# Grouped logits in stacked pairs on eight accumulation banks, and the grouped normaliser in SBUF

## The chip, the cores and the metric

The kernel runs on one core of one Trainium2 chip. The metric is device time in microseconds (us); the kernel before takes 3412.44 us, the median of three runs (3412.42 to 3412.56). A core has a matrix engine (PE, whose weight loads the profile shows as PEld), a vector engine (DVE), a scalar engine (ACT), a slower elementwise engine (POOL) and a queue that issues DMAs (SP). Each works through its own list of instructions in order, and waits on semaphores for the others. PE writes only to PSUM, which here is eight banks of 128 partitions by 512 float32 (2 KB a partition each).

## The reference

Four cross-attention layers are applied in sequence to `x` (4 batches, 512 queries, 256 channels), with the same context `ctx_2048` (4, 1024 keys, 512). Layers 0, 2 and 3 ("masked") have 16 heads of 64; a few key columns get a bias made of two query masks. Layer 1 ("grouped") has an RMS norm ahead, 16 query heads of 16 over 4 key/value heads. Cut to what matters:

```python
def masked(hidden, ctx, mask_A, mask_B, Wq, Wk, Wv, Wo, bo, tokens_A, tokens_B):   # layers 0, 2, 3
    q, k, v = heads_of_64(hidden @ Wq), heads_of_64(ctx @ Wk), heads_of_64(ctx @ Wv)
    logits = einsum('bhqd,bhkd->bhqk', q, k) * 64 ** -0.5 + col_bias   # bias on tokens_A, tokens_B
    out = einsum('bhqk,bhkd->bhqd', softmax(logits), v)
    return merge(out) @ Wo + bo + hidden

def grouped(x, cond, wq, wk, wv, wo, norm_w):                          # layer 1
    q = heads_of_16(rmsnorm(x, norm_w) @ wq)                           # 16 heads, 4 per key head
    scores = einsum('btgrd,bsgd->bgrts', q, k) * 16 ** -0.5
    return x + merge(einsum('bgrts,bsgd->btgrd', softmax(scores), v)) @ wo
```

All is float32.

## The kernel before, in words

**Units and steps.** Work is cut into units of two heads: 8 units for each layer and batch. A unit's logits are 8 blocks of 128 keys by 1024 (two heads of 512 queries), kept in SBUF in one of three sets (`g.st[0..7]`, and a ninth place `g.mx`). `order()` lays the units out in 96 steps: every step has one masked unit `g`, and 32 of them also a grouped unit `lam`: steps 12 to 19, 22 to 29, 32 to 39 and 68 to 75. `coming` is the grouped unit of the step after. Everything below concerns the 28 steps that have both `lam` and `coming` (12-18, 22-28, 32-38, 68-74). Of these, the 16 even ones make values for a pair of masked units (`v_pair`, L605, eight items), the 12 odd ones keys (`k_part`, L552, eight items). Four of the even ones (16, 26, 36, 72) also have a grouped output projection.

**What one such step does on PE, in order.** (1) `scores(g)`: eight tiles of masked logits (L869, the first with a small bias product, L875), each in a place of two banks, copied to SBUF by ACT (L879). (2) `attend` (L902) of the masked unit of the step before, with a place of one bank. (3) A list `fill` of items: output projections (L1108), the next queries (L766), then values or keys, until their estimated times reach 8.0 or 9.5; then `sums_beside` (L1074, the masked unit's softmax sums) and `attend_grouped` (L902 again, 128 by 32 products, into a place of one bank that `keep_even` (ACT, L912) and `keep_odd` (DVE, L916) empty). (4) The grouped logits of `coming`: `logits_pair` (L842) makes two blocks from four products of 32 rows each, which PE runs side by side, in two places of two banks. There are four such pairs. A planner with due times (`pairs`, 12 + 2.5 i) puts the first after `attend_grouped`, and each other one behind one more item of values or keys.

**After a pair.** ACT copies each block to SBUF (L848), which frees its banks, and DVE takes the block's maximum (`block_max`, L926). Behind the fourth pair, `max_quarters` (L942 to L953, seven small DVE instructions in one more PSUM bank) and `max_everywhere` (L966) make the maximum over all keys; POOL subtracts it in the next step (L972). Behind `attend_grouped` of every second grouped unit (`h` = 1, the odd steps), `turn_grouped` divides the unit's output by its sums: three DVE instructions over a PSUM bank (L1029 to L1031) and a product (L1035).

**Banks.** `Place` gives banks out while the program is built. It takes the free place that was given back longest ago in program order, not in time. In these steps two-bank places come from banks 0 to 5, those of `logits_pair` (`last=2`) from banks 0 to 3; one-bank places come from banks 4 to 7. An instruction that reuses a bank waits until the last reader of that bank has finished.

```python
    def max_quarters(g):
        ...
            w = Place(1)
        quarter, half = w.ap[:, 0:32], w.ap[0:64, 32:64]
```

## Time and profile before

| what | value |
|---|---|
| median of three runs | 3412.44 us |
| profiled execution: its time / its span | 3414.65 us / 3412.9 us |
| PE busy | 3397.2 us (100%) |
| DVE / POOL / ACT busy | 2957.4 us (87%) / 2594.2 us (76%) / 2348.5 us (69%) |
| granted PE clock | 0.999 |

A row of a group or a timeline gives the start (timelines only), the duration, the engine, the line of the kernel, the operation with its tiles and shapes, and the count of instructions merged. Matmuls are pipelined, so starts are compared with starts. A float32 product of the kernel is two PE instructions, so a pair of four products shows as x8. The span starts with the first instruction; the profiled execution's time has 1.75 us more than its span.

### The profile page before, as it was taken

How to read it: one execution, taken by the hardware profiler on the slowest of the kernel's cores; microseconds unless marked ns; L12 is line 12 of the kernel's file. 1: busy time of each engine (PE TensorE's matmuls, PEld its weight loads, DVE VectorE, ACT ScalarE, POOL GpSimd, SP SyncE). 2: the span in 40 equal slices, each digit the busy share in tenths (PEclk: the TensorE clock that was granted, in tenths of full speed). 3: DMA queues.
4: the chain of work that ended last, by engine and by line, in shares of the span. 5: the costliest groups of instructions: out<-in, count | busy, mean ns of one | idle time of the engine just before them, and what ended most of it. 6: DMA issues, size and time to landing. Idle time of an engine off the chain costs nothing.

```text
span 3412.9 us, 42703 instructions
## 1 busy us (share of the span) xinstructions
PE 3397.2 (100%) x15520; PEld 1651.6 (48%) x15520; DVE 2957.4 (87%) x3871; ACT 2348.5 (69%) x2729; POOL 2594.2 (76%) x1337
## 2 busy tenths in 40 slices
PE   9999999999999999999999999999999999999999
PEld 5555444444444444445455454554444445454554
DVE  7888799988999889987988889888899988889887
ACT  5666688776787768876666666666678776666665
POOL 4888588875888768888668768677588888769675
PEclk9999999999999999999999999999999999999999
DMA  3232211011101121001001110011111101011100
GB/s 103 69 109 82 65 38 51 30 48 38 55 27 30 48 62 30 27 30 54 19 28 53 35 47 31 28 53 56 38 30 52 36 21 53 28 48 49 34 30 10
DMA packets 147733, 151.69 MB, mean 44 GB/s; under 512 B 23608, under 2 KB 125496, under 8 KB 147012
## 3 DMA queue, kind: packets, MB, share of 16 engines
q1 hardware_dynamic: 144958, 140.58, 13.2%
q0 software_dynamic: 2560, 8.39, 0.8%
q8 instruction: 123, 2.02, 0.2%
q14 instruction: 86, 0.70, 0.1%
q10 hardware_dynamic: 6, 0.00, 0.0%
HBM read 132.15 MB, written 15.73 MB: 43 GB/s over the span
## 4 chain that ended last, share of the span: by engine, by line
PE 93%; DVE 5%; ACT 1%; issue 1%; POOL 0%; DMA 0%; DVEq 0%; ACTq 0%; POOLq 0%
PE ps L902 21%; PE ps L665 18%; PE ps L869 18%; PE ps L552 9%; PE ps L605 9%; PE ps L1108 5%; PE ps L766 5%; PE ps L842 4%; DVE ps L886 2%; DVE st L974 1%; PE ps L1074 1%; PE ps L567 1%; PE ps L875 1%; ACT st L879 1%; PE ps L781 0%
## 5 line engine op out<-in xcount | busy, mean ns | idle before, releaser
L1019 POOL TENSOR_TENSOR st<-st 128x1024 f32<-128x1024 f32 x668 | 1582.2, 2369 | 562.8 <-ACT st L980 518.3
L980 ACT ACTIVATE st<-st 128x1024 f32<-128x1024 f32 x1024 | 1042.1, 1059 | 228.0 <-POOL st L972 118.0
L974 DVE TENSOR_TENSOR st<-st,ps 128x1024 f32<-128x1024 f32 x768 | 884.3, 1215 | 3.3
L902 PE MATMUL ps<-st,v 128*64 128x512 f32 (+1 forms) x4064 | 789.8, 595 | 0.0
L972 POOL TENSOR_TENSOR st<-st 128x1024 f32<-128x1024 f32 x256 | 598.1, 2379 | 211.9 <-DVE st L966 106.0
L879 ACT COPY st<-ps 128x1024 f32<-128x1024 f32 x768 | 713.1, 1050 | 55.3 <-PE ps L875 55.2
L886 DVE TENSOR_TENSOR ps<-ps,st 128x1024 f32<-128x1024 f32 x420 | 517.9, 1233 | 212.3 <-ACT st L879 174.6
L926 DVE TRANSPOSE_TENSOR_REDUCE tops<-st 128x32 f32<-128x1024 f32 x544 | 628.4, 1212 | 69.3 <-ACT st L848 64.6
L869 PE MATMUL ps<-qt,kt 64*128 64x512 f32 x3008 | 687.2, 596 | 0.0
L902 PEld LDWEIGHTS ps<-st,v 128*64 128x64 f32 (+1 forms) x4064 | 239.8, 130 | 535.2 <-issue 448.6
L869 PEld LDWEIGHTS ps<-qt,kt 64*128 64x128 f32 x3008 | 280.4, 186 | 345.5 <-ACT st L879 147.6
L605 PE MATMUL ps<-wv,ctx 128*128 128x256 f32 x1344 | 313.7, 385 | 1.1 <-ACT ctx L428 1.1
L665 PE MATMUL ps<-st 128*128 128x128 f32 (+1 forms) x1620 | 308.8, 339 | 3.7 <-ACT ps L688 3.4
L552 PE MATMUL ps<-ctx,wk 128*128 128x512 f32 x672 | 310.8, 603 | 0.2 <-ACT ctx L428 0.2
L605 PEld LDWEIGHTS ps<-wv,ctx 128*128 128x128 f32 x1344 | 251.0, 191 | 93.1 <-issue 54.9
L848 ACT COPY st<-ps 128x1024 f32<-128x1024 f32 x256 | 247.0, 1018 | 62.3 <-PE ps L842 58.4
L665 PEld LDWEIGHTS ps<-st 128*128 128x128 f32 x1620 | 214.3, 192 | 96.3 <-issue 86.6
L680 ACT COPY st<-ps 128x512 f32<-128x512 f32 x45 | 26.4, 586 | 339.2 <-PE ps L665 339.2
L552 PEld LDWEIGHTS ps<-ctx,wk 128*128 128x128 f32 x672 | 121.7, 189 | 181.0 <-issue 163.6
L766 PE MATMUL ps<-x,wq 128*128 128x512 f32 x376 | 180.4, 602 | 1.3 <-ACT x L391 1.1
L1108 PE MATMUL ps<-ot,wo 128*128 128x512 f32 x380 | 173.2, 598 | 0.0
L842 PE MATMUL ps<-qt,kt 32*128 32x512 f32 x1024 | 160.0, 640 | 0.0
(200 smaller groups left out, 2955.8 us busy)
## 6 DMA issues: line engine op xcount, KB each, us to landing
wv<-in_L_xattn_Wv_dram SPq DMA_DIRECT2D x48, 512.0 KB
ctx<-kept SPq DMA_DIRECT2D x24, 1024.0 KB
wk<-in_L_xattn_Wk_dram SPq DMA_DIRECT2D x47, 512.0 KB
wo<-in_L_xattn_Wo_dram SPq DMA_DIRECT2D x96, 128.0 KB
wq<-in_L_xattn_Wq_dram SPq DMA_DIRECT2D x94, 128.0 KB
st<-kept SPq DMA_DIRECT2D x4, 2048.0 KB
qt<-q SPq DMA_DIRECT2D x64, 128.0 KB
kept<-st SPq DMA_DIRECT2D x12, 512.0 KB
```

What stands on the lines that cost most here:

```text
L552: nc.tensor.matmul(m, lhsT=g.w["k"][:, k, :], rhs=ctx_half[g.b, n][:, k, :], start=(k == 0), stop=(k == KT - 1),)
L605: nc.tensor.matmul(m[:, half * 2 * P : (half + 1) * 2 * P], lhsT=ctx_half[g.b, t // 4][:, k, t % 4 * P : (t % 4 + 1) * P], rhs=g.w["v2"][: ...
L665: nc.tensor.matmul(m if is_keys else m[:, q], lhsT=right[:, k, :] if is_keys else left_[:, k, q], rhs=left_[:, k, :] if is_keys else right ...
L869: nc.tensor.matmul(m[:, j * S : (j + 1) * S], lhsT=g.kt[g.rows[j], keys], rhs=g.qt[g.rows[j], :], start=True, stop=t > 0,)
L879: nc.scalar.copy(g.st[t], m)
L886: nc.vector.tensor_tensor(top, top, g.st[t], ALU.max)
L902: nc.tensor.matmul(g.po[at, :], lhsT=g.v[:, t, rows], rhs=g.st[t][:, j * S : (j + 1) * S], start=(t == first), stop=(t == last),)
L926: nc.vector.tensor_reduce(out_, of.rearrange("p (b x) -> p b x", x=32), AX.X, op, apply_transpose=True)
L972: nc.gpsimd.tensor_tensor(g.st[t], g.st[t], g.mb, ALU.subtract)
L974: nc.vector.tensor_tensor(g.st[t], g.st[t], g.mb, ALU.subtract)
L980: nc.scalar.activation(st, st, AF.Exp)
L1019: nc.gpsimd.tensor_tensor(g.acc, g.st[0] if t == 1 else g.acc, g.st[t], ALU.add)
```

## The change

In the 28 steps, the four pairs of grouped logits are no longer spread by due times. Two pairs stand directly behind `attend_grouped`, then two items of values or keys, then the other two pairs. Their banks come from a fixed list, `PAIR_BANKS`: the first two pairs on banks 0-3 and 4-7, the others on banks 2-5 and 6, 7, 0, 1. The one-bank places of the values or keys behind each two pairs come from a list of hints: banks 0, 1, then 2, 3. `max_quarters`, which is called inside the second two pairs, finds the list empty and takes its bank by the old rule. An odd number of value or key items ahead of the first pairs is made even: in the odd steps and in steps 16, 26, 36 and 72 one item more stands before `attend_grouped`. The exponential of the masked unit's last block moves from behind the first pair to behind the second. `turn_grouped` works in `g.mx` (SBUF) in place of the PSUM bank, which `keep_odd` now always gives back.

```diff
-        def __init__(self, width=2, last=2, among=(4, 5, 6, 7)):
+        def __init__(self, width=2, last=2, among=(4, 5, 6, 7), at=None):
             free = given_back
-            if width == 2:
+            if at is not None or width == 1 and hinted:
+                at = hinted.pop(0) if at is None else at
+            elif width == 2:
...
-    def logits_pair(g, i):
-        ws = [Place(), Place()]
+    PAIR_BANKS = ((0, 2), (4, 6), (2, 4), (6, 0))
+
+    def logits_pair(g, i, fixed):
+        ws = [Place(at=PAIR_BANKS[i][odd] if fixed else None) for odd in range(2)]
...
         nc.vector.tensor_tensor(half, half, g.po[64:128, :], ALU.add)
-        if g.h == 0:
-            g.place.back()
+        g.place.back()
...
     def turn_grouped(g):
-        normalise_grouped(g, g.place.ap)
-        g.place.back()
+        normalise_grouped(g, g.mx[:, 0:S])
...
-            logits_pair(coming, i)
-            if by_ones and events:
+            logits_pair(coming, i, bool(lam))
+            if by_ones and events and i == (1 if lam else 0):
                 events.pop(0)[2]()
...
-            while where < len(fill) and total < (8.0 if by_ones and of_values else 9.5):
+            enough = 8.0 if coming and of_values else 9.5
+            while where < len(fill) and total < enough:
                 total += fill[where][0]
                 where += 1
+            if coming:
+                where += sum(each in of_values + of_keys for each in fill[:where]) % 2
+
+                def two_pairs(bank):
+                    hinted.clear()
+                    pair(pairs.pop(0)[1])
+                    pair(pairs.pop(0)[1])
+                    hinted.extend(range(bank, bank + 2))
+
+                fill.insert(where + 2, (2.0, lambda: two_pairs(2)))
+                fill.insert(where, (2.0, lambda: two_pairs(0)))
             fill.insert(where, (3.6, attend_grouped))
...
-            while pairs and pairs[0][0] <= now:
+            while pairs and not lam and pairs[0][0] <= now:
...
         while pairs:
             pair(pairs.pop(0)[1])
+        hinted.clear()
```

More of the change, by code (lines that the diff above doesn't have):

```diff
@@ L101 @@
     tabled = [False]
+    hinted = []
     class Place:
-        def __init__(self, width=2, last=2, among=(4, 5, 6, 7)):
+        def __init__(self, width=2, last=2, among=(4, 5, 6, 7), at=None):
             free = given_back
-            if width == 2:
+            if at is not None or width == 1 and hinted:
+                at = hinted.pop(0) if at is None else at
+            elif width == 2:
                 whole = [n for n in range(0, 8, 2) if n in free and n + 1 in free]
@@ L1444 @@
             of_queries.append((1.7, lambda: project_q(follows)))
+        of_keys = []
         if fast_k:
@@ L1458 @@
         else:
-            fill += of_queries
-            if kk:
-                fill += keys(*kk)
+            of_keys = keys(*kk) if kk else []
+            fill += of_queries + of_keys
         of_values = values(g) if g and g.n % 2 == 0 and not fast_v else []
```

## The prediction

> **What bounds the kernel.** I read the page first (busy shares, chain of waits), then PE's timeline, then those of ACT, DVE and POOL in one even and one odd step, and last PE's own waits. The page:

> ```profile
> PE 3397.2 (100%) x15520; PEld 1651.6 (48%) x15520; DVE 2957.4 (87%) x3871; ACT 2348.5 (69%) x2729; POOL 2594.2 (76%) x1337
> ...
> PE 93%; DVE 5%; ACT 1%; issue 1%; POOL 0%; DMA 0%; DVEq 0%; ACTq 0%; POOLq 0%
> ```

> PE has about 16 us idle in 3412.9, so a microsecond added to or taken from PE's list is a microsecond of the result. PE's timeline from the first grouped pair of an even step (14 us):

> ```profile
> 450.88 1.14 PE L842 MATMUL ps<-qt,kt 32*128 32x512 f32 x8
> 451.95 1.99 PE L605 MATMUL ps<-wv,ctx 128*128 128x256 f32 x8
> 453.88 1.33 PE L842 MATMUL ps<-qt,kt 32*128 32x512 f32 x8
> 455.14 1.99 PE L605 MATMUL ps<-wv,ctx 128*128 128x256 f32 x8
> 457.06 1.15 PE L842 MATMUL ps<-qt,kt 32*128 32x512 f32 x8
> ...
> 463.25 1.13 PE L869 MATMUL ps<-qt,kt 64*128 64x512 f32 x4
> 464.22 0.38 PE L875 MATMUL ps<-aug_q,aug_k 64*128 64x512 bf16 x2
> 464.43 6.17 PE L869 MATMUL ps<-qt,kt 64*128 64x512 f32 x28
> ```

> From start to start a pair costs 1.07 or 1.26, an item behind it 1.92. The same items in a row (32 of them from 439.30 to 446.30) cost 1.75 each, so a change of product shape costs about 0.17. The pairs at 1.26 (1.35 in odd steps) wait 0.2 to 0.3 for a copy that frees one of their four banks. Next DVE and ACT in the same stretch, and DVE and POOL in an odd step:

> ```profile
> 451.63 0.69 DVE L916 TENSOR_TENSOR o<-o,ps 64x512 f32<-64x512 f32 x1 [1.73 <-ACT o L912]
> 453.15 2.37 DVE L926 TRANSPOSE_TENSOR_REDUCE tops<-st 128x32 f32<-128x1024 f32 x2 [0.82 <-ACT st L848]
> ...
> 462.34 2.37 DVE L926 TRANSPOSE_TENSOR_REDUCE tops<-st 128x32 f32<-128x1024 f32 x2 [0.63 <-ACT st L848]
> 464.75 0.61 DVE L942 TENSOR_REDUCE ps<-tops 128x32 f32<-128x256 f32 x1
> ...
> 466.25 0.38 DVE L953 TENSOR_TENSOR every<-ps,other_max 64x32 f32<-64x32 f32 x2
> 466.74 1.25 DVE L966 STREAM_TRANSPOSE st<-every 128x1024 f32<-128x1024 f32 x1
> 467.91 4.58 DVE L926 TRANSPOSE_TENSOR_REDUCE tops<-st 128x32 f32<-128x1024 f32 x4
> ```

> ```profile
> 452.10 1.93 ACT L848 COPY st<-ps 128x1024 f32<-128x1024 f32 x2 [0.50 <-PE ps L842]
> 453.92 1.07 ACT L980 ACTIVATE st<-st 128x1024 f32<-128x1024 f32 x1
> ```

> ```profile
> 486.78 17.05 POOL L1019 TENSOR_TENSOR st<-st 128x1024 f32<-128x1024 f32 x7
> ```

> The reader is to see that L942 to L953 (the small maximum in a PSUM bank) end at 466.63, 3.4 us after the next step's first score tile starts. Today they use bank 6 or 7 here, which no score tile uses, so nothing on PE waits for them.

> **The change, part by part.** T is the start of the first pair; all step times are from T. The kernel before starts the second score tile of the next step at T + 13.55 in the 12 plain even steps (464.43 - 450.88), at T + 15.31 in the odd ones (14.13 to the first tile, 1.18 on), and at T + 15.36 in the four even steps with a projection.

> *Stacking, what it saves.* The instruction orders of the two kernels show two shape changes in place of four. Four products side by side stream at 0.43 (L902's 32 products of 128 by 32 take 3.57, so eight take 0.89), so the second pair of a stack would cost 0.87 in place of a pair at 1.07 to 1.35. Two items behind a stack cost 1.92 + 1.75 = 3.67 in place of 3.85. Without any wait, an even step would shrink from 12.37 to 2 x (1.07 + 0.87 + 3.67) = 11.2.

> *Wait 1, the grouped output's bank.* The bank that `place_out` gives the grouped output is 7, 6 or 4, and the second pair now wants all of banks 4-7. Its product there waits for L916, which ends at 452.32, T + 1.44. With 0.1 for the release and 1.02 for the last product (a held-up pair ends so much after its release), the items start at T + 2.55, not 1.94; bank 0, which they need, is free by then (first copy ends at T + 2.2). PE's queue behind that product is everything, so 0.6 is lost. The second stack starts at T + 2.55 + 3.67 = T + 6.22. It needs bank 0 again: the item's copy, behind the moved exponential (1.07), ends near T + 6.9, when the fourth pair gets there at T + 7.1. Nothing is lost, with 0.2 to spare.

> *Wait 2, the bank of the small maximum.* Inside the second stack the give-back order hands `max_quarters` bank 4, and in all 28 following steps a score tile is placed on banks 4, 5 directly behind banks 0, 1 (in steps 14 and 74 first of all). In the program of the changed kernel that tile waits for the second half of L953. When does it end? The stack's first copy starts 1.22 after the stack (452.10 - 450.88), its first maximum 1.05 later (453.15): T + 8.49. Four maxima in a row take 4.58. From the last maximum's end (464.71) to the end of L953 (466.63) is 1.92. So bank 4 is free at T + 14.99 and the tile starts at T + 15.07. PE would be there sooner: the items behind the second stack wait for bank 2 until T + 8.5, the first tile starts at T + 12.2, the second could at T + 13.35. PE waits 1.7. Behind it is all of PE's list; DVE, ACT and POOL then stand 2 us earlier against PE, so nothing else turns late and nothing is given back.

> *Sum without the turn.* Plain even steps: 15.07 - 13.55 = +1.52, 12 times, 18.2. In the other 16, one item more (1.75) stands ahead of T. Even with projection: 16.82 - 15.36 = +1.46, 4 times, 5.8. Odd: the item pairs cost 3.65, so 1.75 + 15.05 = 16.80, less 15.31 = +1.49, 12 times, 17.9. Steps 13 and 73 have transposes or a store ahead and the bank-4 tile first: 0.3 more each. Sum +42.5.

> *The turn in SBUF.* L1029 to L1031 work from SBUF to SBUF: 711 to 727 ns either way (L807 against L1029), so nothing. The product L1035 (688 ns) now reads both inputs from SBUF, while POOL is in its seven adds. In an odd step DVE goes from L916 to its first maximum in 3.15, then does eight in 9.13: the bank is free at T + 15.03 by this way too, so each microsecond more here is one on PE. The rows bound it: no delay (L830, both inputs in SBUF, 748 ns, POOL idle), or a whole POOL add of 2.37 waited for. Of the two nearest rows L1035 lacks the second SBUF input and L830 lacks a busy POOL, so neither speaks for its end; I take half an add, 1.2, 12 times: +14.4. Ends 0 and 28.4.

> [...]

> [...]

> *All else*: the four last grouped steps (19, 29, 39, 75) only move the turn, under DVE's idle time. DMAs and POOL's list are the same. **Sum: +42.5 + 14.4 = +56.9.** On the profiled execution 3414.65 this is 3471.6; that execution is 2.2 above the median, so against the median: 3469.

> **Rivals.** *A, the bank comes in time (other side).* If four maxima and L942 to L953 took under 4.8 in place of 6.5 behind the second stack's first copy, wait 2 would go. Then the first tile starts at T + 12.2 in place of 12.37, and about 0.17 to 0.28 is won per step: 3406. Without wait 1 as well (items from T + 2.28, when bank 0 is free, 0.27 sooner in 28 steps): 3398; with no wait at all, 3380. For it: DVE idles 0.6 to 0.8 between maxima today. Against: the copies of one stack come every 0.97, faster than maxima (1.14), so four queue up. *B, dearer.* If the turn is delayed by a whole add and the second pair restarts as a pair of its own (1.07 + 0.2 more, 28 times, 5 us): 3412.4 + 42.5 + 28.4 + 5 = 3488. Against: POOL's adds start at a fixed distance. *C, wait 2 alone*, the turn free: 3455; this is the low end of the forecast. *D, it cancels*: the shape changes might cost more than 0.17; to cancel +42.5, stacks would have to save 1.5 more each step than the 1.16 of the ideal. Not likely.

> **How the numbers follow.** Forecast (waits 1 and 2, any turn between C and a full add: 3455 to 3483) 0.88; A 0.04; B 0.05; D 0.03. Two runs of this kernel can be told apart from about 0.2%, 7 us. Faster 0.04, same 0.03, slower 0.93. The range: C's 3455 less 0.3 of wait 1 and 0.2 of DVE's chain in 28 steps, 14, gives 3441; the full add gives 3483.

> **What would show it.** In the profile after: PE's first idle time in score tiles, 28 waits of 1.5 to 3 us for the line of L953; PE busy below 98.5%; pairs as x16 from start to start 1.9 (no wait 1) or 2.55; L1035's duration far over 688 in odd steps if the turn is held. The prediction is wrong if those 28 waits are missing, or if the stall is given back where today's kernel waits on something that I take for PE's own work.

## The result, and the profile after

The changed kernel takes 3489.11 us, the median of four runs (3486.09 to 3491.34); the kernel before beside it took 3412.43 us. The ratio is 1.0223, interval 1.0210 to 1.0235: slower by 76.7 us, where 56.6 were predicted. The direction is right, the time is 20 us above the forecast and 6 us above the range's upper end. The profiled execution took 3486.09 us with a span of 3484.0 us, which is 71.1 us more than the span before. In the changed file the lines of the code have moved by three to five: L842 is L847, L869 is L874, L916 is L921, L926 is L930, L953 is L957, L1035 is L1038.

The page after: busy times, the chain of waits by engine, and the group of the score tiles.

```profile
PE 3398.3 (98%) x15520; PEld 1665.5 (48%) x15520; DVE 2971.0 (85%) x3871; ACT 2344.9 (67%) x2729; POOL 2593.5 (74%) x1337
...
PE 84%; DVE 13%; ACT 2%; issue 1%; POOL 0%; DMA 0%; DVEq 0%; ACTq 0%
...
L874 PE MATMUL ps<-qt,kt 64*128 64x512 f32 x3008 | 702.3, 607 | 61.3 <-DVE every L957 61.3
```

PE does the same work in nearly the same busy time, and what was added is, by these sums, idle time. (The sums hide two opposite changes: the pairs and the items between them take less, and the score tiles 702.3 us where they took 687.2.) The list of PE's waits (total, times, longest) names it:

```profile
PE ps L874 <- DVE every L957: 61.3, 28, 3.2
PE ps L608 <- ACT st L853: 4.7, 16, 0.3
PE ps L555 <- ACT st L853: 3.5, 12, 0.3
```

These are the 28 waits of the prediction, one for each step, for the small maximum. PE's timeline of an even step, the same one that the prediction shows, and DVE's beside it:

```profile
449.06 2.61 PE L847 MATMUL ps<-qt,kt 32*128 32x512 f32 x16
451.60 3.72 PE L608 MATMUL ps<-wv,ctx 128*128 128x256 f32 x16
455.25 2.00 PE L847 MATMUL ps<-qt,kt 32*128 32x512 f32 x16
457.55 3.72 PE L608 MATMUL ps<-wv,ctx 128*128 128x256 f32 x16 [0.29 <-ACT st L853]
461.20 1.13 PE L874 MATMUL ps<-qt,kt 64*128 64x512 f32 x4
462.16 0.38 PE L880 MATMUL ps<-aug_q,aug_k 64*128 64x512 bf16 x2
464.18 6.28 PE L874 MATMUL ps<-qt,kt 64*128 64x512 f32 x28 [1.64 <-DVE every L957]
```

```profile
457.53 4.62 DVE L930 TRANSPOSE_TENSOR_REDUCE tops<-st 128x32 f32<-128x1024 f32 x4 [1.58 <-ACT st L853]
462.25 0.59 DVE L946 TENSOR_REDUCE ps<-tops 128x32 f32<-128x256 f32 x1
...
463.74 0.38 DVE L957 TENSOR_TENSOR every<-ps,other_max 64x32 f32<-64x32 f32 x2
```

The two stacks of pairs are shorter, as predicted: 2.54 from start to start with wait 1 in it, then 2.00 and 0.29 of wait for bank 2. The second score tile starts 15.12 after the first pair, where 15.07 was predicted. The four maxima queue behind the second stack, and PE stands until the small maximum behind them has left bank 4.

An odd step has the same wait with the turned product ahead of it. Timelines of PE, DVE and POOL:

```profile
597.11 1.13 PE L874 MATMUL ps<-qt,kt 64*128 64x512 f32 x4
...
601.30 9.29 PE L874 MATMUL ps<-qt,kt 64*128 64x512 f32 x28 [2.84 <-DVE every L957]
610.52 7.09 PE L907 MATMUL ps<-st,v 128*64 128x512 f32 x32
```

```profile
588.34 1.90 DVE L1038 TENSOR_TENSOR o<-o,st 128x512 f32<-128x512 f32 x1
590.17 9.12 DVE L930 TRANSPOSE_TENSOR_REDUCE tops<-st 128x32 f32<-128x1024 f32 x8
```

```profile
575.09 14.61 POOL L1023 TENSOR_TENSOR st<-st 128x1024 f32<-128x1024 f32 x6
```

The sixth POOL add ends at 589.70, 1.36 us after the product (L1038) has started, and the product ends 0.54 us behind it. It takes 1.90 us, 1.2 more than before, and 2.84 is 1.64 + 1.20. So far everything is as forecast. What the forecast does not have stands in the second row: behind this wait the seven score tiles take 9.29 us, where the same ones took 6.28 in the even step. The next view cuts that time in two at 607.40; its columns are busy time and instructions of PE, PEld, DVE, ACT and POOL, the granted clock of PE, DMA share and GB/s.

```profile
601.30:607.40 6.10, 6.10 (x14) 2.55 (x16) 4.82 (x4) 2.58 (x3) 4.73 (x3) 0.50 0.00 0
607.40:610.50 3.10, 3.10 (x16) 1.14 (x12) 2.64 (x4) 2.89 (x4) 3.10 (x2) 1.00 0.00 0
```

For the first 6.1 us the granted clock is 0.50, and 14 PE instructions fall in it where 16 fall in the next 3.1 us. The clock's record has six such stretches between the first and the last of the 28 steps, four of 3.41 us and two of 6.83 us, 27.3 us in all; before, none lies there. The odd steps behind which they stand are longer than their like by 1.4 to 3.0 us, 12.2 us together. So the result has two parts: the predicted waits, and a loss of clock behind some of them. The four runs of the changed kernel spread over 5.3 us, while those before stay within 0.2. Their granted clock is 0.996, 0.995, 0.994 and 0.994, so the amount of low clock differs from run to run; only the first was profiled.

### The profile page after: what moved, and what is told of

Same layout as the page of the kernel before. It is cut to its first block, busy times and chain, and to the rows that moved or that the text cites. A ratio compares the mean times of both kernels' runs of the same rounds, so it can differ in the third digit from the quotient of the medians.

```text
span 3484.0 us, 42527 instructions
## 1 busy us (share of the span) xinstructions
PE 3398.3 (98%) x15520; PEld 1665.5 (48%) x15520; DVE 2971.0 (85%) x3871; ACT 2344.9 (67%) x2729; POOL 2593.5 (74%) x1337
## 4 chain that ended last, share of the span: by engine, by line
PE 84%; DVE 13%; ACT 2%; issue 1%; POOL 0%; DMA 0%; DVEq 0%; ACTq 0%
PE ps L907 21%; PE ps L668 18%; PE ps L874 18%; PE ps L608 6%; PE ps L555 6%; DVE tops L930 5%; PE ps L1111 5%; PE ps L769 5%; PE ps L847 2%; DVE ps L891 2%; DVE st L978 1%; PE ps L1077 1%; PE ps L570 1%; DVE o L1038 1%; DVE ps L946 0%
## 5 line engine op out<-in xcount | busy, mean ns | idle before, releaser
L984 ACT ACTIVATE st<-st 128x1024 f32<-128x1024 f32 x1024 | 1039.1, 1060 | 171.3 <-DVE st L978 102.4
L976 POOL TENSOR_TENSOR st<-st 128x1024 f32<-128x1024 f32 x256 | 597.6, 2375 | 247.1 <-DVE st L970 209.1
L874 PE MATMUL ps<-qt,kt 64*128 64x512 f32 x3008 | 702.3, 607 | 61.3 <-DVE every L957 61.3
L930 DVE TRANSPOSE_TENSOR_REDUCE tops<-st 128x32 f32<-128x1024 f32 x544 | 624.5, 1208 | 64.6 <-ACT st L853 50.6
L874 PEld LDWEIGHTS ps<-qt,kt 64*128 64x128 f32 x3008 | 283.3, 189 | 423.5 <-issue 150.8
L608 PE MATMUL ps<-wv,ctx 128*128 128x256 f32 x1344 | 303.5, 382 | 5.8 <-ACT st L853 4.7
L847 PE MATMUL ps<-qt,kt 32*128 32x512 f32 x1024 | 147.8, 621 | 1.4 <-DVE o L921 1.4
```

The costliest lines, as they stand in the source:

```text
L608: nc.tensor.matmul(m[:, half * 2 * P : (half + 1) * 2 * P], lhsT=ctx_half[g.b, t // 4][:, k, t % 4 * P : (t % 4 + 1) * P], rhs=g.w["v2"][: ...
L874: nc.tensor.matmul(m[:, j * S : (j + 1) * S], lhsT=g.kt[g.rows[j], keys], rhs=g.qt[g.rows[j], :], start=True, stop=t > 0,)
L930: nc.vector.tensor_reduce(out_, of.rearrange("p (b x) -> p b x", x=32), AX.X, op, apply_transpose=True)
L976: nc.gpsimd.tensor_tensor(g.st[t], g.st[t], g.mb, ALU.subtract)
L984: nc.scalar.activation(st, st, AF.Exp)
```

## The experiments

The kernel before, run beside the experiments, had medians of 3413.6 to 3413.8 us; every ratio is to these. The theory: the 28 waits are for the bank of the small maximum (wait 2), the turn adds its delay to 12 of them, and the clock falls behind the longest. The rivals: the stall has another source and comes back when bank 4 is freed; the turn is free; the low clock comes from something other than the length of the wait.

**1. The small maximum on bank 7**, which no score tile uses.

```diff
-    def max_quarters(g):
+    def max_quarters(g, at=None):
...
-            w = Place(1)
+            w = Place(1, at=at)
...
-                max_quarters(coming)
+                max_quarters(coming, 7 if lam else None)
```

> The changed kernel, but the small maximum behind the second stack takes bank 7 in place of bank 4 (28 steps), so no score tile shares its bank. Theory (the loss is the wait for bank 4, made longer in odd steps by the held product, plus half clock after the longest waits): the 28 waits for L957's line go, the half-clock stretches go with them, the first tile starts at T + 12.15 in place of 12.37, and 7 us are won on the kernel before: 3405 us if nothing else turns late. What may turn late next: the odd steps' maximum, still behind the held product, starts POOL's subtraction some 2 us later against PE than in the kernel before, and the next step's grouped attend may wait up to 1.4 us for it, 16 times: up to 3427. Rival (stacking itself is dear, by wait 1 or by ACT's copies in fours): most of the loss stays, over 3455.

Measured: 3435.2 us, ratio 1.0061 (1.0044 to 1.0077). All 28 waits are gone, and of the 76.7 us some 21 are left, so wait 2 is shown to be their cause. But it is not the gain that this run was expected to bring, for in the even steps another wait took their place. PE's list of waits, PE's timeline of one even step, and ACT's and DVE's just before:

```profile
PE ps L847 <- DVE o L921: 12.6, 12, 1.3
```

```profile
703.56 2.32 PE L847 MATMUL ps<-qt,kt 32*128 32x512 f32 x14
707.19 1.12 PE L847 MATMUL ps<-qt,kt 32*128 32x512 f32 x2 [1.30 <-DVE o L921]
708.24 5.39 PE L608 MATMUL ps<-wv,ctx 128*128 128x256 f32 x16
```

```profile
703.94 2.00 ACT L984 ACTIVATE st<-st 128x1024 f32<-128x1024 f32 x2
705.85 0.57 ACT L917 COPY o<-ps 64x512 f32<-64x512 f32 x1
```

```profile
706.45 0.69 DVE L921 TENSOR_TENSOR o<-o,ps 64x512 f32<-64x512 f32 x1 [1.73 <-ACT o L917]
```

With PE not held up, ACT is now behind it: the exponentials (L984) that stand ahead of `keep_even` (L917) run late, `keep_odd` (L921) follows, and the last product of the second pair waits 1.30 us for its bank. That is wait 1 grown. Five of these waits are followed by the low clock; the items of values that take 3.72 us elsewhere take 5.39 here, with a granted clock of 0.51 from 708.20 to 711.60. Rival A of the prediction (the bank in time: 3398 to 3406) thus has its condition met, and its price was wrong.

**2. The turned product on POOL**, so that it can't meet a POOL add on the way to the maximum.

```diff
-        nc.vector.tensor_tensor(o, o, m, ALU.mult)
+        nc.gpsimd.tensor_tensor(o, o, m, ALU.mult)
```

> The changed kernel, but the product that ends the turn (output times reciprocals, both in SBUF) runs on POOL in place of DVE. Theory: DVE loses the held 1.9 us in odd steps, so the odd waits for bank 4 fall from 2.84 to the even steps' 1.64; no wait is long enough for a half-clock stretch; 12 x 1.2 and the clock's 14 us go: 3455 us, with runs within 1 us of each other. Rival (half clock follows any wait of 1.6 us, or the stacks themselves): half-clock stretches stay, 3460 to 3475. Rival (the product was not held, DVE was late for another cause): odd waits stay over 2.1.

Measured: 3463.85 us, ratio 1.0147 (1.0130 to 1.0164). The list of PE's waits has the 28 waits with the delay of the product gone from the odd ones; they are 1.63 to 1.66 us in all but three steps:

```profile
PE ps L874 <- DVE every L957: 47.2, 28, 2.1
```

The profiled run has no stretch of low clock, and its span of 3458.2 is 45.3 above the one before, where the prediction's sum without the turn is 42.5. So the turned product on DVE costs some 26 us in the changed kernel (76.7 - 50.1): 14 by its delay (61.3 against 47.2 us of waits), the rest, by subtraction, by the clock. By its number the run lies 9 us above the theory and in the range of the first rival, but the profiled run shows no stretch of that rival, and a part of the 9 are the small amounts that the prediction missed (below). The other three runs are about 3.5 us slower than the profiled one; three waits of 2.01 to 2.07 are left, and low clock behind them would explain it, which no profile shows.

**3. The turn in SBUF alone**, in the kernel before.

```diff
-        normalise_grouped(g, g.place.ap)
+        normalise_grouped(g, g.mx[:, 0:S])
```

> The kernel before, with one part of the change alone: the turn works in SBUF (the ninth place of the unit's set) while the PSUM bank is kept as long as before. Theory: the product L1035, in the same place beside POOL's adds with only the home of one operand changed, goes from 688 ns to between 1.2 and 2.9 us; nothing on PE waits for DVE there, so 3412 us, or up to 3424 if POOL's later start makes the next grouped attend late. Rival (the hold belongs to the stacks): the product stays at about 690 to 750 ns, 3412 us.

Measured: 3414.19 us, ratio 1.0001 (0.9991 to 1.0011). Here the product reaches DVE just as a POOL add ends: it takes about 0.70 us in 12 of 16 places and is held in four, for 2.00 to 2.03, and no product of PE waits for it. The edit costs nothing alone; it costs what it does because the stacks move it against the adds and put the DVE chain on PE's path.

**4. One idle product in the 28 waits**, to see whether the clock falls because PE stands. It goes to bank 7, 128 by 512, and nothing reads it.

```diff
+            if t == 0 and stacked[0]:
+                warm = Place(1, at=7)
+                nc.tensor.matmul(warm.ap, lhsT=ones, rhs=g.qt, start=True, stop=True)
+                warm.back()
...
+            stacked[0] = bool(lam and at(n - 1)[1])
```

> The changed kernel, with one idle product (128 by 512, written to bank 7 and never read) on PE between the first score tile and the one that waits, in the 28 steps; it adds work and takes no wait away. Theory (PE's clock halves after an idle time near 3 us): the tile behind still starts when bank 4 comes, idle times fall to about 0.6 and 1.8, the half-clock stretches go, and the time falls to 3412.4 + 56.9 = 3469 us with runs within 1 us. Rival (the slow stretches come from something else, such as ACT or DVE at the same banks): they stay, 3480 to 3495.

Measured: 3486.6 us, ratio 1.0212 (1.0195 to 1.0229): no gain clear of the spread, and a time in the rival's range. Nine of the odd waits still left PE idle for 1.75 to 1.79 us, one for 2.15, and behind two odd steps (in the scores of steps 14 and 74) the wait of 3.2 us stands ahead of the first tile and wasn't filled at all. Five stretches of low clock stay. The expectation took it that shortening would do; it had no length from which it does.

**5. Two idle products, in the odd waits only**, ahead of the first tile in the two steps where that one waits.

```diff
+            def fill_wait():
+                warm = Place(1, at=7)
+                for _ in range(stacked[0]):
+                    nc.tensor.matmul(warm.ap, lhsT=ones, rhs=g.qt, start=True, stop=True)
+                warm.back()
+
+            if t == 0 and stacked[0] and w.banks[0] == 4:
+                fill_wait()
...
+            if t == 0 and stacked[0] and w.banks[0] != 4:
+                fill_wait()
...
+            stacked[0] = 2 if lam and at(n - 1)[1] and at(n - 1)[1].h else 0
```

> The changed kernel with two idle products of 128x512 to bank 7 in each odd-step wait only (before the first score tile where that one waits). It adds no work on the path, since PE stands there anyway; the idle part of the odd waits falls from 2.84 us to about 0.9 (about 1.3 in steps 14 and 74), while the even ones keep their 1.64. Theory (the clock halves only after a window of 3.41 us in which PE stood for more than about 1.75 us): no half-clock stretch is left, the three runs agree within about 1 us, and the time is that of the predicted sum alone, 3412.8 + 56.9 = 3470 (3466 to 3473). Rival (the half-clock stretches come from something else in the step, such as the slow weight loads): they stay, and the time is 3480 to 3490.

Measured: 3475.13 us (3474.68 to 3475.18), ratio 1.0180 (1.0163 to 1.0197). The runs agree within 0.5 us, and the clock's record has no low stretch between the start and the end. PE's timeline of the same odd step as above:

```profile
596.71 1.13 PE L884 MATMUL ps<-qt,kt 64*128 64x512 f32 x4
...
597.98 1.98 PE L878 MATMUL ps<-qt,ones 128*128 128x512 f32 x4
600.89 6.28 PE L884 MATMUL ps<-qt,kt 64*128 64x512 f32 x28 [0.93 <-DVE every L969]
```

The second tile starts as long after the first as in the changed kernel (600.89 - 596.71 = 4.18 here, 601.30 - 597.11 = 4.19 there), yet the tiles behind it take 6.28 us instead of 9.29. This kernel waits as long and computes more, and loses 61.5 us (3475.13 - 3413.63) where the changed one loses 76.7. So the clock falls here because PE stands idle, and 61.5 is the price of the waits without it. It is 2 us above the range of the expectation, which took the prediction's sum for exact; the theory of the cause holds.

**6. Bank 7 and the product on POOL together**, from the two edits shown in 1 and 2.

> The changed kernel with two edits: the second half maximum stands on bank 7 (as in the run with that edit alone) and the 16 products of the turned sums are POOL's. Theory: what kept the run with bank 7 alone at 3435 was the chain product late, maximum late, POOL's subtraction late, ACT's exponentials late, keep_even and keep_odd of the next even step late. With the product on POOL the DVE is free about 0.75 us earlier (0.6 of product, and the rest of the lock), the even steps' second stack shrinks from 3.8-5.4 towards 2.5, its products wait 0.4 us or less, and the clock falls to half in no step or one: 3405 to 3418. Rival: POOL's 16 products of 1.28 us push its own subtractions back by as much, the exponentials stay late, and the time is 3420 to 3436 with half-clock stretches left.

Measured: 3425.24 us, ratio 1.0033 (1.0021 to 1.0046): in the rival's range, with stretches of low clock left as it said.

```profile
PE ps L847 <- DVE o L921: 8.3, 12, 1.3
PE ps L608 <- ACT st L853: 4.7, 16, 0.3
PE ps L555 <- ACT st L853: 3.5, 12, 0.3
```

Of the 12 waits for `keep_odd` six are 0.17 to 0.35 and six still 1.02 to 1.31, and three of these are followed by the low clock (the items behind them take 5.41 us where they take 3.72 behind the others). What the expectation calls the lock the runs show as a time alone: beside POOL's adds the product took 1.86 to 1.91 us in the 12 odd steps of the changed kernel, where it took 0.69 before; that anything is locked no run shows. The rival's cause is not what the trace shows: POOL stands idle for at least 5.6 us ahead of each of its series of subtractions (L976), so its products are not what makes these late. The copies that free bank 2 late cost 8.2 us more in 28 steps, as in the changed kernel. With the wait for bank 4 and the held product out of the way, the stacked order is still not faster than the spread one.

**7. The banks without the stacks.** The kernel before, its pairs spread as they were, but over three sets of banks; single users keep to banks 4 and 5.

```diff
+            if narrow[0] and among == (4, 5, 6, 7):
+                among = (4, 5)
...
-    def logits_pair(g, i):
-        ws = [Place(), Place()]
+    PAIR_BANKS = ((0, 2), (6, 0), (2, 6), (0, 2))
+
+    def logits_pair(g, i, fixed):
+        ws = [Place(at=PAIR_BANKS[i][odd] if fixed else None) for odd in range(2)]
...
+            narrow[0] = bool(lam)
+            logits_pair(coming, i, bool(lam))
...
+                max_quarters(coming, 6 if lam else None)
```

> The kernel before, without stacking, with only the list of banks taken over: in the 28 steps the four pairs stand on the banks 0-1 and 2-3, 6-7 and 0-1, 2-3 and 6-7, 0-1 and 2-3, the score tiles and what else takes two banks in these steps on 4-5, and the second half maximum on bank 6. Theory: the pairs' stalls of 0.19 to 0.28 us each (pairs that took 1.26, 1.27 and 1.35 where an unhindered one takes 1.07) go, 0.39 in the 12 even and 0.48 in the 12 odd steps and 0.47 in the 4 with a projection, and nothing new waits: -12.3, 3400 to 3404. Rival: single users squeezed on banks 4-5 make a new wait of 0.4 us or more a step: 3410 or above.

Measured: 3423.92 us, ratio 1.0030 (1.0019 to 1.0040). All 28 steps lose the pairs' stalls (every pair but one, under low clock, 1.07 us from start to start), and the even ones are shorter by just the 0.39 and 0.47 that were expected. But in the odd steps the second pair waits, and the trace lays it to the copy of the keys; PE's waits, and DVE's timeline just before such a wait, which on PE ends at 913.52:

```profile
PE ps L850 <- ACT kt L563: 14.2, 8, 2.0
PE ps L850 <- ACT st L988: 4.3, 4, 1.1
```

```profile
912.68 0.69 DVE L1043 TENSOR_TENSOR o<-o,ps 128x512 f32<-128x512 f32 x1
```

The program has that pair on bank 6, which the turned sums leave with this product, at 913.37. A copy or an exponential on ACT ends 0.02 us before the pair starts, and the list names what came last. But in all 12 such waits the pair starts 0.147 to 0.148 us after the product's end, whichever of the two the list names.

**8. The same, with the second pair of the odd steps on its old banks.**

```diff
-    PAIR_BANKS = ((0, 2), (6, 0), (2, 6), (0, 2))
+    PAIR_BANKS = ((0, 2), (6, 0), (2, 6), (0, 2)), ((0, 2), (0, 2), (6, 0), (2, 0))
...
-            logits_pair(coming, i, bool(lam))
+            logits_pair(coming, i, 1 + lam.h if lam else 0)
```

> As the rotation without stacking, but the 14 odd steps give the second pair the banks 0-1 and 2-3 as before, so that it doesn't meet the bank 6 of the turned sums, and take 6-7 for the third pair alone. Theory (the 1.06 to 2.03 us wait of the second pair in the odd steps of the rotation was for the turned product on bank 6): that wait goes, the even steps keep their saving (19.26 for 19.65 us twelve times, 20.99 for 21.46 four times), the odd steps lose the third pair's stall of 0.28 us twelve times, and no half-clock stretch is left: -4.7 - 1.9 - 3.4 = -10, 3403 to 3405. Rival (the wait was for the copy of the keys, as the trace's label has it, because of the banks 4 and 5 that the single users now share): it stays at 1 to 2 us in the odd steps, and the time is 3415 to 3425.

Measured: 3408.17 us, ratio 0.9984 (0.9975 to 0.9993): 5.5 us faster than the kernel before, the only version here that beats it. The long waits are gone with the bank, while the single users are still on banks 4 and 5, so it was the turned product. An even and an odd step of PE's timeline:

```profile
534.51 1.14 PE L850 MATMUL ps<-qt,kt 32*128 32x512 f32 x8
535.58 1.99 PE L611 MATMUL ps<-wv,ctx 128*128 128x256 f32 x8
537.51 1.14 PE L850 MATMUL ps<-qt,kt 32*128 32x512 f32 x8
```

```profile
578.86 1.55 PE L850 MATMUL ps<-qt,kt 32*128 32x512 f32 x8
...
585.23 1.37 PE L850 MATMUL ps<-qt,kt 32*128 32x512 f32 x8
```

The even steps keep their saving (every pair 3.00 from the next, where two in four stood 3.18 apart). The odd ones win nothing: the third pair's stall is gone, the fourth pair (1.30 from start to start in all 12) stalls more than before, and the second does in eight (1.46 to 1.48 in seven, 1.74 in one; it was 1.27). That is the 3 to 5 us by which the expectation was too good.

## Why the prediction was right or wrong

*Stacking, what it saves* holds. The stacks take 2.54 and 2.00 us, against 2.55 and 1.07 + 0.87 = 1.94.

*Wait 1* holds in the changed kernel: L921 ends 1.44 us after the first pair (449.06 to 450.50), and the items start after 2.54.

*Wait 2* holds: 1.64 us in the even steps where 1.7 was predicted, the second tile at 15.12 where 15.07 was. Two small amounts were missed: 0.05 in this start, and 0.11 in the seven tiles behind it (6.28 against 6.17; in run 5 in 26 of the 28 steps). From one step's sums (`sums_beside`, L1089 there) to the next's in the run with the odd waits filled, without the item that is moved (1.72), a plain even step costs 1.67 more than before (predicted 1.52), a projection step 1.60 (1.46), an odd step 2.80 (1.49 + 1.2). That makes 12 x 1.67 + 4 x 1.60 + 12 x 2.80 = 60, with the remainder in the steps of the longer first wait.

*The turn in SBUF* holds in its size by half an accident. The choice of half an add, 1.2, was the author's estimate, the middle between the bounds, and no row of the kernel before shows a product held by an add. The runs do: the product took 1.89 us in the median where it had 0.69, 1.20 more, because in the odd steps of this order it reaches DVE about 1.35 us ahead of an add's end, and it ends 0.55 us behind that end.

The 56.9 of the sum thus compare with the 61.5 of the run without low clock. **The step that failed** is the last sentence of wait 2, "Behind it is all of PE's list; DVE, ACT and POOL then stand 2 us earlier against PE, so nothing else turns late and nothing is given back", together with the sum that follows from it. It prices a wait on PE at its own length. The runs show a further term: behind some of the idle waits PE runs at a granted clock of 0.50 for 3.41 or 6.83 us. In the profiled run of the changed kernel, which is 3 us faster than its median, this is 12.2 us; by the medians it is 15.2 (76.7 - 61.5). The error of the forecast is thus 15.2 for the clock and 4.6 for the small amounts above. The range failed with the same term: its upper end was a whole add in the turn, and it held no price for the clock, though the profile before has one low stretch of 3.41 us (granted clock 0.50), 18.1 us from its start, that shows what the clock can do.

Of the rivals, A's condition was made true by run 1 and gave 3435, not 3398 to 3406, since wait 1 grows once wait 2 is gone. B, 3488, is near the measured time by its number and not by its cause: the product took 1.90 and not 3.06, and no pair started anew. C, the turn free, 3455, is run 2 at 3463.85, dearer by the missed amounts and, as it seems, some clock. D did not occur. How many banks are in use doesn't tell the versions apart: the kernel before already uses all eight in these steps, though not for the pairs. Stacks on all eight are still 11.6 us slower with both delays taken away (run 6), and a gain came from giving the spread pairs banks 6 and 7 as well (run 8).

## What to carry to other kernels

A wait on PE may not be over when it ends: in a kernel that keeps PE at 100%, give a price to the time behind it at a low clock as well (here 0.50 for 3.41 or 6.83 us behind six of 28 waits). When such a wait can't be taken away, idle products in it can help: here they took 15 us off when they cut the odd waits to 1.5 us and less (run 5), and nothing clear when they left 1.75 and more (run 4). Before an engine's work is pulled together to save switches, ask which slow chain will hold the resources that it now takes at once: here eight banks in one go cost a wait of 1.6 us, and of the ideal saving of about 1.2 only 0.23 was left at the first score tile of an even step (461.20 - 449.06 = 12.14 after the first pair, in place of 12.37). A rotation over more banks with the work left spread won, once it kept clear of the bank that the turned sums hold. Here the price of a DVE product with both inputs in SBUF, beside POOL's adds in SBUF, followed what was left of the add when the product started: it was nothing in 12 of 16 places in one order (run 3) and 1.2 us in the odd steps of another (the changed kernel).

## What the runs showed of the hardware

**The held product.** In the changed kernel and in runs 1 and 3, the turned product's duration follows from what is left of the POOL add in progress when it starts, plus about 0.55 us, with 0.69 as the least, for all 48 products: 1.35 us left gave 1.90, 0.62 gave 1.17, 0.84 gave 1.39, 1.46 gave 2.01, 0.09 gave 0.69. An add that starts while such a product runs takes 2.67 to 2.74 us instead of 2.36; one that starts later takes 2.36. With one input in PSUM the same product took 686 to 690 ns in all 16 places of the kernel before and of runs 7 and 8, with up to 1.6 us of an add left.
